# The first layernorm of sequences 1 to 15 taken from transposed input instead of through TensorE

## The chip, the cores and the metric

The kernel runs on one core of one Trainium2 chip. The metric is the device time of one launch in microseconds (us). The kernel before was timed in three runs: 996.58 us median, 995.12 us lowest, 997.07 us highest.

## The reference

The reference is a block of a conditioned transformer on 16 sequences of 256 tokens with 256 channels, in float32, with 16 heads of 64 and 8 experts of width 1024. Cut to what matters:

```python
def _ln(x, g, b):
    m = jnp.mean(x, axis=-1, keepdims=True)
    v = jnp.var(x, axis=-1, keepdims=True)
    return (x - m) * jax.lax.rsqrt(v + EPS) * g + b
shift = silu(t) @ W_ada.T + b_ada
h = _ln(x, ln1_g, ln1_b) + shift            # the first layernorm
qkv = (h @ Wqkv.T).reshape(b, n, 3, H, HD)
q, k = _ln(q-part, qn_g, qn_b), _ln(k-part, kn_g, kn_b)   # per head
attn = softmax(q @ k.T / sqrt(HD))
x = x + (attn @ v) @ Wout.T
tok = x.reshape(-1, d)
gate = softmax(tok @ Wgate.T)
vals, idx = top_k(gate.T, bs // E)          # each expert takes 512 tokens
g = _ln(tok[idx], mlp_g, mlp_b)
y = gelu(g @ fc1 + b1) @ fc2 + b2
tok = tok.at[idx].add(y * w)
```

The change concerns the line of `h` alone: the mean and the rate 1/sqrt(v + EPS) belong to a token, the gain `ln1_g` and the shift (`ln1_b` plus `shift`) to a channel.

## The kernel before, in words

**Stages.** The first part of the program works through the 16 sequences; the second routes tokens to experts and runs the experts' two matmuls, job by job. In the first part every sequence needs its normalised input `hT` with channels on partitions (two chunks of 128 channels, 256 tokens each), since TensorE contracts over partitions. From `hT` come the q, k and v rows in six groups of 512 columns for two halves of 128 tokens (`Group`, tile `pm`). Then come the normalisation of q and k on ScalarE, VectorE and GpSimd, their turn into channel order, the scores (`Quad.scores`, tile `sc`), the exponentials, their normalisation on GpSimd (`Quad.normalise`, tile `pr`), a turn of 32x32 blocks on VectorE (`pb`) with four DMAs that deal the blocks to partitions (`exchange`, tile `prT`), the product with v (`po`), and the output projection with the gate logits (`Tail.project`, tile `pw`).

**The first layernorm before** is the class `First`. VectorE takes mean and variance of the 256 channels of a token (L639, L640, tokens on partitions, input `xs`). GpSimd raises variance plus EPS to the power -1/2 (L644, and `rsqrt` at L102). VectorE applies both (L651, tile `xn`). TensorE turns the result in four 128x128 blocks (L660, into a PSUM tile `ph` with the tag "mm", of which there are three tiles for `pm`, `ph`, `pq`, `pw` and half of `po`). ScalarE evicts it with gain and shift of the channel into `hT` (L673). A tile `xT`, the raw input with channels on partitions, is loaded as well, for the gate logits in `Tail.project`; there are two such tiles.

**Shapes of the array.** TensorE runs in three shapes. `halved` (L496 to L500) splits a 128x128 weight into two 128x64 halves, for `pm`, `pw` and the like; `product` (L920) uses 128x64 too; `scores` (L834) uses quarters of 64x64; transposes use all 128x128. Except in transposes, every float32 matmul of the program shows as two records in the trace, so 16 rows of the program's order are 32 records.

**The order.** The program is written as a list of steps (`plan.step`, called `at`): a nominal place, an engine, a duration, the function, what it needs and makes, and the tiles it holds. A table of numbers, `PLACES`, one for each step, fixes the order in which all steps are issued (`Plan.order`, used at L1800). Each engine and each DMA queue works through its own steps strictly in that order, and each instruction waits for what it needs. The SyncE queue (SP) issues the loads of `xs` and `xT`, the exchanges and the stores of the tokens.

Of the kernel before, what the change touches and what calls it, by code (L numbers as in the profile page):

```python
# [63 lines left out]
def kernel(  # L64
# [115 lines left out]
    def make_others():  # L180
# [287 lines left out]
    if True:  # L468
# [161 lines left out]
        class First:  # L630
# [18 lines left out]
            def apply(self, t):  # L649
                self.xn[t] = work.tile([P, D], F32, tag="xn", bufs=4, name="xn")  # L650
                nc.vector.tensor_scalar(  # L651
                    self.xn[t], xs[self.b][:, t, :], self.mv[:, 0, t : t + 1],
                    self.rs[:, 1, t : t + 1], ALU.subtract, ALU.mult,
                )

            def transposes(self):
                self.pt = turned_in("ph", self.b == 0)
# [1287 lines left out]
```

## Time and profile before

| | |
|---|---|
| median of three runs | 996.58 us |
| the profiled execution's own time | 994.14 us |
| its span, first to last instruction | 992.3 us |
| PE (TensorE) busy | 974.5 us, 98% |
| DVE (VectorE) busy | 788.0 us, 79% |
| POOL (GpSimd) busy | 652.3 us, 66% |
| ACT (ScalarE) busy | 595.1 us, 60% |

The span ends 1.84 us short of the profiled execution's time. That execution is 2.44 us below the median of the runs. Shares are of the whole span; the two parts of the program load the engines differently, so they are read by stretch. In the listings, matmuls overlap their neighbours, so what a group costs TensorE is read from the distance between the start of one group and the start of the next, rather than from the busy time of the group.

### The profile page before, as it was taken

How to read it: one execution, taken by the hardware profiler on the slowest of the kernel's cores; microseconds unless marked ns; L12 is line 12 of the kernel's file. 1: busy time of each engine (PE TensorE's matmuls, PEld its weight loads, DVE VectorE, ACT ScalarE, POOL GpSimd, SP SyncE). 2: the span in 40 equal slices, each digit the busy share in tenths (PEclk: the TensorE clock that was granted, in tenths of full speed). 3: DMA queues.
4: the chain of work that ended last, by engine and by line, in shares of the span. 5: the costliest groups of instructions: out<-in, count | busy, mean ns of one | idle time of the engine just before them, and what ended most of it. 6: DMA issues, size and time to landing. Idle time of an engine off the chain costs nothing.

```text
span 992.3 us, 22827 instructions
## 1 busy us (share of the span) xinstructions
PE 974.5 (98%) x7732; PEld 583.4 (59%) x7732; DVE 788.0 (79%) x1919; ACT 595.1 (60%) x1684; POOL 652.3 (66%) x1069
## 2 busy tenths in 40 slices
PE   9999999999999999999999999999999999999996
PEld 5444544444454545444454544455577888899995
DVE  6788888988899899898899899989964666477661
ACT  2788675757766676666667676766773432344441
POOL 4688677768687767777676777776535345455653
PEclk9999999999999999999999999999999999999998
DMA  8024567667576776576676667777734665766672
GB/s 289 1 55 96 139 155 170 153 166 189 144 176 166 185 189 164 127 174 172 162 179 160 170 156 184 179 176 178 180 108 145 212 181 160 218 187 183 196 220 31
DMA packets 153667, 160.56 MB, mean 162 GB/s; under 512 B 16080, under 2 KB 146640, under 8 KB 153552
## 3 DMA queue, kind: packets, MB, share of 16 engines
q1 hardware_dynamic: 145152, 148.68, 55.6%
q0 software_dynamic: 7168, 8.53, 5.1%
q10 hardware_dynamic: 1232, 1.90, 0.6%
q8 instruction: 62, 1.02, 0.4%
q14 instruction: 53, 0.43, 0.1%
HBM read 53.94 MB, written 12.84 MB: 67 GB/s over the span
## 4 chain that ended last, share of the span: by engine, by line
PE 82%; POOL 5%; DVE 4%; DMA 3%; issue 2%; SPq 2%; ACT 1%; POOLq 0%; DVEq 0%
PE pm L500 28%; PE ph L1427 10%; PE po L920 10%; PE sc L834 10%; PE pw L500 9%; PE seven L1483 5%; PE py L1443 5%; POOL ss L102 2%; DMA prT<-pb 2%; SPq L594 1%; POOL pr L867 1%; PE pp L898 1%; PE ph L660 1%; PE fill L489 1%; PE px L1396 1%
## 5 line engine op out<-in xcount | busy, mean ns | idle before, releaser
L500 PE MATMUL pm<-wq,hT 128*64 128x512 f32 x1536 | 350.6, 595 | 1.0 <-DVE qk L749 0.6
L867 POOL TENSOR_SCALAR pr<-pr,sums 128x256 f32<-128x256 f32 x512 | 236.8, 480 | 81.0 <-DVE sums L863 69.3
L856 ACT ACTIVATE pr<-sc,nmax 128x256 f32<-128x256 f32 x512 | 237.4, 479 | 84.3 <-DVE nmax L843 69.0
L102 POOL TENSOR_TENSOR ss<-ss,neghalf 128x8 f32<-128x8 f32 x128 | 210.4, 1644 | 10.6
L500 PEld LDWEIGHTS pm<-wq,hT 128*64 128x64 f32 x1536 | 108.1, 137 | 181.5 <-issue 153.2
L843 DVE TENSOR_REDUCE nmax<-sc 128x2 f32<-128x512 f32 x256 | 166.3, 669 | 6.5 <-PE sc L834 6.0
L877 DVE STREAM_TRANSPOSE pb<-pr 128x512 f32<-128x512 f32 x232 | 156.7, 690 | 16.1 <-POOL pr L867 8.8
L725 ACT ACTIVATE sq<-pm 128x512 f32<-128x512 f32 x128 | 77.0, 603 | 86.9 <-PE pm L500 83.9
L920 PE MATMUL po<-prT,v 128*64 128x256 f32 x1024 | 126.1, 381 | 1.6 <-DMA prT<-pb 1.2
L834 PE MATMUL sc<-kT,qT 64*64 64x256 f32 x2048 | 126.6, 383 | 0.1
L500 PE MATMUL pw<-wo,oT 128*64 128x264 f32 x1024 | 126.2, 389 | 0.2
L1427 PE MATMUL ph<-xT,w 128*128 128x256 f32 x512 | 117.2, 383 | 0.8 <-ACT xT L1414 0.7
L920 PEld LDWEIGHTS po<-prT,v 128*64 128x64 f32 x1024 | 73.3, 137 | 63.3 <-issue 28.1
L856 ACT ACTIVATION_READ_ACCUMULATOR pr<-sc,nmax 128x1 f32 x512 | 108.0, 211 | 0.0
L834 PEld LDWEIGHTS sc<-kT,qT 64*64 64x64 f32 x2048 | 72.5, 132 | 60.3 <-issue 21.6
L749 DVE TENSOR_TENSOR qk<-pm,ss 128x512 f32<-128x512 f32 x128 | 90.0, 704 | 19.1 <-POOL ss L102 17.9
L729 DVE TENSOR_REDUCE ss<-sq 128x8 f32<-128x512 f32 x128 | 85.5, 669 | 24.7 <-ACT sq L725 23.8
L1427 PEld LDWEIGHTS ph<-xT,w 128*128 128x128 f32 x512 | 94.2, 190 | 13.9 <-ACT xT L1414 1.6
L1434 ACT ACTIVATE hid<-ph,few 128x256 f32<-128x256 f32 x128 | 60.2, 473 | 66.0 <-PE ph L1427 61.8
L500 PEld LDWEIGHTS pw<-wo,oT 128*64 128x64 f32 x1024 | 71.3, 137 | 38.6 <-issue 5.2
L1377 POOL DMA_INDIRECT xg<-xn_dram,idx x32 | 33.7, 1054 | 85.6 <-DVE idx L1370 31.2
L781 DVE STREAM_TRANSPOSE kb<-qk 128x512 f32<-128x512 f32 x120 | 82.8, 693 | 1.8 <-DMA prT<-pb 0.6
(212 smaller groups left out, 1112.0 us busy)
## 6 DMA issues: line engine op xcount, KB each, us to landing
prT<-pb SPq DMA_DIRECT2D x464, 128.0 KB, 2.6
w<-in_fc2T SPq DMA_DIRECT2D x16, 1024.0 KB, 6.2
w<-in_fc1T SPq DMA_DIRECT2D x16, 1024.0 KB, 9.1
qraw<-kb SPq DMA_DIRECT2D x120, 128.0 KB, 2.6
kT<-kb SPq DMA_DIRECT2D x120, 128.0 KB, 2.7
xs<-in_x SPq DMA_DIRECT2D x16, 256.0 KB, 3.3
xT<-in_xT SPq DMA_DIRECT2D x16, 256.0 KB, 3.2
out<-tok SPq DMA_DIRECT2D x32, 128.0 KB, 2.5
```

The source lines that it names most:

```text
L102: nc.gpsimd.tensor_tensor(dst, src, neghalf[:, : src.shape[1]], ALU.pow)
L500: nc.tensor.matmul(dst[half], weights[:, half], moving, start=start, stop=stop)
L729: nc.vector.tensor_reduce(self.ss[:, 0, :], self.sq.rearrange("p (q e d) -> p e q d", q=QB, e=8), AX.XY, ALU.add,)
L749: engine.tensor_tensor(dst, src.rearrange("p (q e d) -> p q e d", q=QB, e=8), by_head(self.ss[:, 1, :]), ALU.mult,)
L781: nc.vector.transpose(kb[0][:, :, self.t], self.qk.rearrange("p (q h d) -> p q h d", q=QB, d=SQ),)
L834: nc.tensor.matmul(self.sc[i, j][k * HD : (k + 1) * HD, t, :], qTs[self.b][rows, hp, bass.ts(2 * t + k, HD)], keys[rows, hp] if direct els ...
L843: nc.vector.tensor_reduce(self.nmax[i, j], self.sc[i, j], AX.X, ALU.max, negate=True)
L856: nc.scalar.activation(dst, src, AF.Exp, bias=self.nmax[i, j][:, t : t + 1], scale=1.0, accum_out=self.sums[i][:, 0, j, t : t + 1],)
L867: nc.gpsimd.tensor_scalar(self.pr[i, j][:, t, :], self.pr[i, j][:, t, :], self.sums[i][:, 1, j, t : t + 1], 1.0, ALU.mult, ALU.mult,)
L877: nc.vector.transpose(self.pb[i][:, :, :, j].rearrange("p k c t n -> p t k c n"), self.pr[i, j].rearrange("p t (k c m) -> p t k c m", c=TB ...
L920: nc.tensor.matmul(self.po[j * HD : (j + 1) * HD, i, :], vs[self.b][:, c, bass.ts(4 * self.d + 2 * i + j, HD)], prT[:, j, c] if self.whole ...
L1427: nc.tensor.matmul(self.ph[f], self.w1[:, c, bass.ts(f, P)], self.xT[:, c, :], start=(c == 0), stop=(c == DC - 1),)
```

## The change

For sequences 1 to 15 (sequence 0 keeps the old way) `First` no longer applies mean and rate with tokens on partitions, and TensorE no longer turns the result. Instead:

- GpSimd multiplies mean and rate of each token (`rates`, 128x2).
- VectorE transposes the four columns (mean times rate and rate, for two halves of the tokens), each repeated 32 times, in 32x32 blocks (`lay`, 128x128): every partition of a block of 32 then holds the values of that block's 32 tokens.
- SP deals each of the four blocks of 32 partitions to all 128 partitions by a DMA (`spread`, four per sequence, 64 KB written each).
- GpSimd multiplies `xT` by the rates (`times`) and subtracts mean times rate (`less`), each in two halves of 128x256 elements, into `hT`.
- ScalarE applies gain and shift in place (`shifted`, two instructions of 128x256).

`xT` is loaded earlier and has four tiles instead of two. The PSUM tile `ph` of sequences 1 to 15 is gone, as is the tag "xn" (`xn` of sequence 0 shares the tag "tok"). The table `PLACES` is new throughout, because there are more steps and another order.

```diff
@@ PLACES
-        0, 1, 2, 3, 4, 5, 6, 7, 18, 15, 21, 24, 23, 27, 31, 20, 14, 8, 56, 72, 73, 74, 75,
...
@@ class First
             def apply(self, t):
-                self.xn[t] = work.tile([P, D], F32, tag="xn", bufs=4, name="xn")
+                self.xn[t] = work.tile([P, D], F32, tag="tok", bufs=3, name="xn")
...
+            def rates(self):
+                nc.gpsimd.tensor_tensor(self.rs[:, 0], self.mv[:, 0], self.rs[:, 1], ALU.mult)
+            def lay(self):
+                self.side = work.tile([P, 2 * TB, SQ], F32, tag="side", bufs=2, name="side")
+                nc.vector.transpose(
+                    self.side,
+                    self.rs.rearrange("p k t -> p (k t)").unsqueeze(2).to_broadcast([P, 2 * TB, SQ]),
+                )
+            def spread(self, q):
+                if q == 0:
+                    self.rows = seq.tile([P, QB, 2 * TB * SQ], F32, tag="rows", bufs=2, name="rows")
+                part = self.side[q * SQ : (q + 1) * SQ].rearrange("p w i -> p (w i)")
+                nc.sync.dma_start(
+                    self.rows[:, q], part.unsqueeze(1).to_broadcast([SQ, QB, 2 * TB * SQ])
+                )
+            def along(self, k, t):
+                rows = self.rows.rearrange("p q (k t i) -> p k t q i", k=2, t=TB)[:, k, t]
+                return rows.unsqueeze(1).to_broadcast([P, DC, QB, SQ])
+            def by_block(self, v, t):
+                return v[:, :, bass.ts(t, P)].rearrange("p c (q i) -> p c q i", q=QB)
+            def times(self, t):
+                nc.gpsimd.tensor_tensor(
+                    self.by_block(self.out(), t), self.by_block(xTs[self.b], t), self.along(1, t),
+                    ALU.mult,
+                )
+            def less(self, t):
+                h = self.by_block(self.out(), t)
+                nc.gpsimd.tensor_tensor(h, h, self.along(0, t), ALU.subtract)
+            def shifted(self):
+                h = self.out()
+                for c in range(DC):
+                    nc.scalar.activation(
+                        h[:, c, :], h[:, c, :], AF.Identity,
+                        bias=bias1[:, c, self.b : self.b + 1],
+                        scale=vec[:, LN1_G + c : LN1_G + c + 1],
+                    )
@@ class Tail
-                xTs[self.b] = seq.tile([P, DC, N], F32, tag="xT", bufs=2, name="xT")
+                xTs[self.b] = seq.tile([P, DC, N], F32, tag="xT", bufs=4, name="xT")
@@ the steps of a sequence
+            at(base + FIRST[0] - 19, "SP", 0.64, Tail(b, 0).load, (), [("xT", b)], [("xT", b)], lag=3.0)
...
-                at(base + FIRST[4], "ACT", 0.91, a.evict, [("ht", b), "bias1"], [("hT", b)], [pt, ("hT", b)], lag=0.22)
+                rows, hT = ("lines", b), ("hT", b)
+                at(base + FIRST[1] + 0.1, "POOL", 0.22, a.rates, [("fp", b)], [("fr", b)], [l1])
+                at(base + FIRST[1] + 0.2, "DVE", 0.2, a.lay, [("fr", b)], [("fl", b)], [l1, ("side", b)], lag=0.19)
+                for q in range(QB):
+                    at(base + FIRST[1] + 0.3 + 0.1 * q, "SP", 0.66, partial(a.spread, q), [("fl", b)] + ([("ls", b, q - 1)] if q else []), [rows, ("ls", b, q)], [("side", b), rows], lag=2.2)
+                for t in range(TB):
+                    at(base + FIRST[2] + t, "POOL", 0.68, partial(a.times, t), [rows, ("xT", b)], [("h1", b, t)], [rows, ("xT", b), hT])
+                    at(base + FIRST[2] + t + 0.5, "POOL", 0.68, partial(a.less, t), [("h1", b, t)], [("h2", b)], [rows, hT])
+                at(base + FIRST[4], "ACT", 0.98, a.shifted, [("h2", b), "bias1"], [hT], [hT], lag=0.22)
```

**The order on TensorE** around the scores of sequence 6 and the first scores of sequence 7. `ph` is the turn of sequence 7's normalised input; the numbers behind tile names are those of buffers. Before:

```order
L500 MATMUL pm<-wq,hT_3229 64x512 x16
L834 MATMUL sc<-kT_2886,qT_3092 64x256 x16
L920 MATMUL po<-prT,v_2914 64x256 x4
L500 MATMUL pm<-wq,hT_3229 64x512 x4
L920 MATMUL po<-prT,v_2914 64x256 x4
L500 MATMUL pw<-wo,oT_3330 64x264 x2
L500 MATMUL pw<-few,xT 64x8 x4
L500 MATMUL pw<-wo,oT_3330 64x264 x16
L500 MATMUL pw<-few,xT 64x8 x4
L500 MATMUL pw<-wo,oT_3330 64x264 x14
L660 MATMUL ph<-ident,xn 128x128 x4
L834 MATMUL sc<-kT_3585,qT_3719 64x256 x16
```

The same place with the change:

```order
L525 MATMUL pm<-wq,hT_2995 64x512 x16
L905 MATMUL sc<-kT_3010,qT_3001 64x256 x16
L525 MATMUL pw<-wo,oT_3185 64x264 x2
L525 MATMUL pw<-few,xT 64x8 x4
L525 MATMUL pw<-wo,oT_3185 64x264 x14
L525 MATMUL pm<-wq,hT_2995 64x512 x4
L525 MATMUL pw<-wo,oT_3185 64x264 x2
L525 MATMUL pw<-few,xT 64x8 x4
L525 MATMUL pw<-wo,oT_3185 64x264 x14
L991 MATMUL po<-prT,v_2959 64x256 x4
L905 MATMUL sc<-kT_3636,qT_3687 64x256 x16
```

The four transposes between `pw` and `sc` are gone and nothing has taken their place; the other rows are dealt differently. Elsewhere the new order splits groups of scores. This is sequence 3 with the change:

```order
L905 MATMUL sc<-kT_1903,qT_1968 64x256 x16
L525 MATMUL pm<-wq,hT_1595 64x512 x8
L991 MATMUL po<-prT,v_1206 64x256 x12
L905 MATMUL sc<-kT_1903,qT_1968 64x256 x8
L991 MATMUL po<-prT,v_1206 64x256 x4
L525 MATMUL pm<-wq,hT_1595 64x512 x16
```

A group of 16 there has become two of 8, with other work between them. Up to the first transpose of the routing (`pgT`), the order before has 64 uninterrupted groups of `sc`, two of which are of 8; the new order has 69, twelve of which are of 8. In the routing, six rows of `pw` stand between the first list (`pls`) and the 36 fills ahead of the first `px`, where before the fills came right behind the list.

**The order on GpSimd** around the input of sequence 4 (`hT_1595` with the change; `pr` are the probabilities, which the products wait for; `ss` and `rs` are small powers). With the change:

```order
L709 TENSOR_TENSOR hT_1595<-xT,rows 128x2x128
L636 TENSOR_SCALAR rs<-mv 128x1
L102 TENSOR_TENSOR rs<-rs,neghalf 128x1
L938 TENSOR_SCALAR pr<-pr,sums 128x256 x6
L806 TENSOR_SCALAR ss<-ss 128x8
L102 TENSOR_TENSOR ss<-ss,neghalf 128x8
L806 TENSOR_SCALAR ss<-ss 128x8
L102 TENSOR_TENSOR ss<-ss,neghalf 128x8
L938 TENSOR_SCALAR pr<-pr,sums 128x256 x2
L709 TENSOR_TENSOR hT_1595<-xT,rows 128x2x128
L938 TENSOR_SCALAR pr<-pr,sums 128x256 x2
L716 TENSOR_TENSOR hT_1595<-hT_1595,rows 128x2x128
```

Before, the queue holds probabilities and powers alone in these sequences:

```order
L735 TENSOR_SCALAR ss<-ss 128x8
L102 TENSOR_TENSOR ss<-ss,neghalf 128x8
L611 TENSOR_SCALAR rs<-mv 128x1
L102 TENSOR_TENSOR rs<-rs,neghalf 128x1
L867 TENSOR_SCALAR pr<-pr,sums 128x256 x4
```

The elementwise work on `hT` (L709, L716) now stands between the probabilities, in single pieces or in pairs.

**The order on the SP queue** of the same sequences with the change (`rows` are the dealt rates):

```order
L619 DMA prT<-pb 128x1x256 x4
L697 DMA rows<-side 128x1x128
L507 DMA xs_2884<-in_x 128x2x256
L1094 DMA xn_dram<-tn 128x256
L619 DMA prT<-pb 128x1x256 x4
L697 DMA rows<-side 128x1x128
L1015 DMA xT<-in_xT 128x2x256
L619 DMA qraw<-kb 128x1x256 x4
L697 DMA rows<-side 128x1x128 x2
L619 DMA prT<-pb 128x1x256 x4
```

Sixty issues of `rows` are new, dealt between the exchanges, and the loads of `xT` have moved to earlier places. The whole queue has 856 issues before and 916 with the change.

## Rows read from the trace of the kernel before

**Rows 1.** The page, part 1: busy time, share of the span, instructions.

```profile
PE 974.5 (98%) x7732; PEld 583.4 (59%) x7732; DVE 788.0 (79%) x1919; ACT 595.1 (60%) x1684; POOL 652.3 (66%) x1069
```

**Rows 2.** Windows: length, busy us per engine (instructions), PE clock, DMA share, GB/s.

```profile
60.00:700.00 640.00, 636.57 (x5428) 313.00 (x5426) 569.80 (x1152) 438.51 (x1302) 475.00 (x849) 1.00 0.65 163
...
709.00:753.00 44.00, 41.57 (x454) 29.62 (x455) 30.77 (x136) 28.99 (x94) 16.91 (x37) 1.00 0.41 120
```

**Rows 3.** Waits of PE: line waited for, total us, times, longest.

```profile
PE po L920 <- DMA prT<-pb: 1.2, 3, 0.7
...
PE pm L500 <- DVE qk L749: 0.6, 1, 0.6
PE ph L660 <- DVE gates L1026: 0.5, 1, 0.5
```

**Rows 4.** Timeline of PE near 140 us: start us, us, engine, line, operation, records.

```profile
136.30 3.63 PE L500 MATMUL pm<-wq,hT 128*64 128x512 f32 x16
139.86 0.65 PE L660 MATMUL ph<-ident,xn 128*128 128x128 f32 x4
140.44 1.96 PE L834 MATMUL sc<-kT,qT 64*64 64x256 f32 x32
142.33 1.08 PE L500 MATMUL pm<-wq,hT 128*64 128x512 f32 x4
```

**Rows 5.** Timeline of PE: 48 records of `pm` in a row; scores right behind 16.

```profile
10.32 10.52 PE L500 MATMUL pm<-wq,hT 128*64 128x512 f32 x48
20.67 0.40 PE L500 MATMUL pf<-few,wout 128*64 128x64 f32 x8
...
709.49 3.65 PE L500 MATMUL pm<-wq,hT 128*64 128x512 f32 x16
713.07 1.96 PE L834 MATMUL sc<-kT,qT 64*64 64x256 f32 x32
```

**Rows 6.** Timeline of PE near 86 us: a group of scores half as long.

```profile
85.73 1.09 PE L834 MATMUL sc<-kT,qT 64*64 64x256 f32 x16
86.76 1.08 PE L500 MATMUL pm<-wq,hT 128*64 128x512 f32 x4
```

**Rows 7.** Lines by form, PE: records, busy us, mean ns, idle before, releaser.

```profile
L660 PE MATMUL ph<-ident,xn 128*128 128x128 f32 x64 | 10.8, 294 | 0.5 <-DVE gates L1026 0.5
```

**Rows 8.** Lines by form, POOL.

```profile
L867 POOL TENSOR_SCALAR pr<-pr,sums 128x256 f32<-128x256 f32 x512 | 236.8, 480 | 81.0 <-DVE sums L863 69.3 <-DVE gates L1026 2.8 <-ACT v L721 0.9
L589 POOL TENSOR_TENSOR wq<-wq,ws 128x512 f32<-128x512 f32 x4 | 4.5, 1135 | 0.3
L989 POOL TENSOR_TENSOR tok<-tok,xs 128x256 f32<-128x256 f32 x4 | 2.8, 734 | 0.0
L1081 POOL TENSOR_TENSOR gates<-gates,smax 128x16 f32<-128x16 f32 x1 | 0.2, 212 | 5.3 <-DVE gate_of L1076 5.3
```

**Rows 9.** Lines by form, DVE and ACT.

```profile
L877 DVE STREAM_TRANSPOSE pb<-pr 128x512 f32<-128x512 f32 x232 | 156.7, 690 | 16.1 <-POOL pr L867 8.8 <-DMA qraw<-kb 3.4 <-DMA prT<-pb 2.2
L863 DVE RECIPROCAL sums<-sums 128x4 f32<-128x4 f32 x128 | 19.5, 154 | 7.4 <-ACT pr L856 6.9
L651 DVE TENSOR_SCALAR xn<-xs,mv,rs 128x256 f32<-128x256 f32 x32 | 13.1, 412 | 0.2 <-POOL rs L102 0.2
L673 ACT ACTIVATE hT<-ph,bias,few 128x256 f32<-128x256 f32 x31 | 16.0, 571 | 18.2 <-PE ph L660 18.2
```

**Rows 10.** Timeline of the SP queue near 302 us: four issues of an exchange.

```profile
301.67 2.50 SPq L594 DMA_DIRECT2D kT<-kb  x4
```

**Rows 11.** The page, parts 3 and 6: queue totals, and us to landing.

```profile
q1 hardware_dynamic: 145152, 148.68, 55.6%
...
prT<-pb SPq DMA_DIRECT2D x464, 128.0 KB, 2.6
```

**Rows 12.** Timeline of PE in the routing: `pgT` starts it, `ph` starts the experts.

```profile
708.85 0.71 PE L1109 MATMUL pgT<-ident,gate_of 128*128 128x128 f32 x2
...
733.68 1.56 PE L500 MATMUL pw<-wo,oT 128*64 128x264 f32 x12
735.05 0.38 PE L500 MATMUL pw<-few,xT 128*64 128x8 f32 x8
...
745.89 4.10 PE L489 MATMUL fill<-ident 128*128 128x128 f32 x36
750.18 0.41 PE L1396 MATMUL px<-ident,xg 128*128 128x128 f32 x2 [0.20 <-DMA xg<-xn_dram,idx]
751.34 0.44 PE L1396 MATMUL px<-ident,xg 128*128 128x128 f32 x2 [0.74 <-DMA xg<-xn_dram,idx]
...
752.57 3.72 PE L1427 MATMUL ph<-xT,w 128*128 128x256 f32 x16 [0.68 <-ACT xT L1414]
```

More of the change, by code (lines that the diff above doesn't have):

```diff
@@ L1546 @@
         plan = Plan(dict(
-            mm=3, sc=4, po=1, xs=5, hT=2, qT=2, kT=2, v=2, oT=2, xn=4, sq=2, ss=4, qk=3, nmax=8, aside=4,
-            sums=4, pr=PRB, pb=3, qraw=2, prT=4, tok=3, tn=2, xT=2, pa=1, l1=4, l2=4,
+            mm=3, sc=4, po=1, xs=5, hT=2, qT=2, kT=2, v=2, oT=2, lines=2, side=2, sq=2, ss=4, qk=3, nmax=8, aside=4,
+            sums=4, pr=PRB, pb=3, qraw=2, prT=4, tok=3, tn=2, xT=4, pa=1, l1=4, l2=4,
         ))
@@ L1591 @@
             at(base + FIRST[1], "POOL", 0.92, a.power, [("fs", b)], [("fp", b)], [l1])
-            for t in range(TB):
-                at(base + FIRST[2] + t, "DVE", 0.32, partial(a.apply, t), [("fp", b)], [("xn", b)], [l1, ("xs", b), ("xn", b, t)], lag=0.18)
-            pt = ("mm", b, 0)
-            at(base + FIRST[3], "PE", 0.44, a.transposes, [("xn", b)], [("ht", b)], [pt, ("xn", b, 0), ("xn", b, 1)] + ([("mm", b, 0.1)] if b == 0 else []), lag=0.22)
             if b == 0:
+                for t in range(TB):
+                    at(base + FIRST[2] + t, "DVE", 0.32, partial(a.apply, t), [("fp", b)], [("xn", b)], [l1, ("xs", b), ("tok", "xn", t)], lag=0.18)
+                pt, pt1 = ("mm", b, 0), ("mm", b, 0.1)
+                at(base + FIRST[3], "PE", 0.44, a.transposes, [("xn", b)], [("ht", b)], [pt, ("tok", "xn", 0), ("tok", "xn", 1), pt1], lag=0.22)
                 at(base + FIRST[4], "ACT", 0.56, partial(a.evict, (0,)), [("ht", b), "bias1", "later"], [("hT", b)], [pt, ("hT", b)], lag=0.22)
-                at(base + FIRST[4], "DVE", 0.42, partial(a.evict_too, 1), [("ht", b), "bias1"], [("hT", b)], [("mm", b, 0.1), ("hT", b)], lag=0.19)
+                at(base + FIRST[4], "DVE", 0.42, partial(a.evict_too, 1), [("ht", b), "bias1"], [("hT", b)], [pt1, ("hT", b)], lag=0.19)
             else:
-                at(base + FIRST[4], "ACT", 0.91, a.evict, [("ht", b), "bias1"], [("hT", b)], [pt, ("hT", b)], lag=0.22)
+                rows, hT = ("lines", b), ("hT", b)
[3 more added lines that the diff above has]
+                    at(base + FIRST[1] + 0.3 + 0.1 * q, "SP", 0.66, partial(a.spread, q), [("fl", b)] + ([("ls", b, q - 1)] if q else []), [rows, ("ls", b, q)], [("side", b), rows], lag=2.2)
+                for t in range(TB):
+                    at(base + FIRST[2] + t, "POOL", 0.68, partial(a.times, t), [rows, ("xT", b)], [("h1", b, t)], [rows, ("xT", b), hT])
+                    at(base + FIRST[2] + t + 0.5, "POOL", 0.68, partial(a.less, t), [("h1", b, t)], [("h2", b)], [rows, hT])
+                at(base + FIRST[4], "ACT", 0.98, a.shifted, [("h2", b), "bias1"], [hT], [hT], lag=0.22)
             turned = {g: [] for g in range(4)}
@@ L1669 @@
                 pw, tok, tn, l2 = (("sc", 97) if (b, t) == (B - 1, 1) else ("mm", 4)) + n, ("tok",) + n, ("tn",) + n, ("l2",) + n
-                if t == 0:
-                    at(p - 40, "SP", 0.65, a.load, (), [("xT", b)], [("xT", b)], lag=3.0)
                 need, tile_ = [("oT", b), ("xT", b), "wog"], [pw, ("oT", b), ("xT", b)]
```

486 rows, old and new, of the table PLACES are left out of this document.

## The prediction

> **What bounds the kernel now.** I read the busy shares first, then the windows by stage, then TensorE's waits, and last the timeline around the transposes that the change removes. The shares put TensorE at 98% of the span and the next engine, VectorE, at 79% [rows 1]. A share is no proof of a bound, so the stage that the change touches comes next: from 60 to 700 us TensorE is busy 636.57 of 640 us, VectorE 569.80, GpSimd 475.00 and ScalarE 438.51 [rows 2]. TensorE idles 3.4 us there, all at the full clock (1.00). Its waits in this stage are short and few: 1.2 us in three pieces for `prT`, 0.6 us for `qk`, 0.5 us ahead of one group of `ph` [rows 3]. So in the attention stage an operation taken off TensorE is time taken off the end, as long as the others keep up. From 709 to 753 us TensorE has 2.4 us idle and much fill work, and the search for the thresholds sets the pace [rows 2, 12]. That stage should move as a whole: it begins with `pgT`, when TensorE has got through the same attention work as before.
>
> **The transposes that go.** Fifteen groups of four leave TensorE's order. What one costs is read from starts. A `ph` group that starts at 139.86 is followed by scores at 140.44, which is 0.58 us [rows 4]. Ahead of it, 16 records of `pm` took 3.56 us from their start to `ph`; where scores follow 16 records of `pm` directly, it is 3.58 us [rows 4, 5]. So without the group the way into the scores costs the same as the way into the group did, and the whole 0.58 us is saved: 15 x 0.58 = 8.7 us. Bounds: the group of 64 has 10.8 us of busy time, of which 60/64 is 10.1, with ends that overlap the next work [rows 7]; and 36 fills, transposes of the same size in one run, take 4.10 us, 0.114 each, so 60 of them at that rate are 6.8 us [rows 12]. I take 8.7, since it was read at the place itself.
>
> **What the new order gives back on TensorE.** Scores stand in 64 uninterrupted groups before `pgT` in the old order and in 69 in the new one, so five more splits. A whole group takes 1.89 us to the start of the next work, half a group 1.03 [rows 4, 6]: two halves cost 2.06, 0.17 more. Entering scores costs something too: 48 records of `pm` in a row take 10.35 us, 0.216 each, so 16 should take 3.45, and took 3.58 before scores [rows 5]. That is 0.13 more per entry. Five splits at 0.30 are +1.5 us. The Trainium skill's page "TensorEngine Tiling (Array Packing)", section Key Properties, says that changing the tiling mode drains TensorE. The 0.13 and 0.17 us agree with it. The rule speaks against the new order, not against the removal: by it alone one would credit each removed group with a change of shape as well, 15 x 0.13 = 2.0 us more and a sum of -7.3 in place of the -5.3 below, while the rows show the entry into `ph` replaced by an equal entry into the scores.
>
> **GpSimd.** Per sequence come four two-input instructions of 128x256 and a small one. The nearest rows are 734 ns for 128x256, and 1135 ns for 128x512 with a broadcast operand, 568 for half of it [rows 8]. I take 0.65, between the two, and 0.21 for the small one [rows 8]: 2.8 us per sequence, 42 us in all (37 to 47). Nothing leaves GpSimd. Hence 475 of 640 us, 74%, becomes about 516 of 633, 82%. By itself this is beside TensorE; what it costs is lateness of `pr`, on which `pb`, the exchange and `po` hang, because pieces of `hT` now stand ahead of it in the queue.
>
> **VectorE and ScalarE.** VectorE loses two applications of 0.41 us per sequence and gains one block transpose of 128x128, bounded by 0.15 (the smallest instruction shown) and 0.69 (four times the elements); I take 0.3, nearer to the small one since it has a quarter of the elements [rows 9]. That is 0.5 us less per sequence on an engine at 89% in this stage, so nothing lost. ScalarE's two instructions of 0.57 us [rows 9] stay, reading SBUF instead of PSUM: no term, between -0.1 and +0.1 us each, and hidden, as ScalarE is at 69% there. One user of the three "mm" tiles goes, which can only relax TensorE; no term.
>
> **SP and the transfers.** Four more issues per sequence at 0.6 us (four took 2.50) are 2.4 us of SP's queue [rows 10], 36 us in all, hidden as long as exchanges behind them land in time. Each writes 64 KB; by packets of 512 B, 60 x 128 are 7,680 on top of 145,152, which took 55.6% [rows 11], so about 3 points more if a small packet costs as much as the mean one. An exchange lands in 2.6 us [rows 11]; I leave it there. The first DMA of `rows` waits for `lay`, and the exchanges of `prT` queue behind it. The earlier `xT` loads are the same bytes at other times; those of the first sequences stand ahead of some weights, which could cost up to about 1 us early on (256 KB; issue gaps of 0.6 us), taken as 0.
>
> **Waits that I add.** TensorE's idle time in the stage is 3.4 us now. GpSimd's busy time over its free time goes from 475/165 = 2.9 to 516/117 = 4.4, half as much again. If TensorE's idle time grows in proportion, that is +1.7; I take +1.6 us, an estimate, with 0 and 7 as bounds (7: half a microsecond in each of 15 sequences).
>
> **The routing.** Six rows of `pw`, 12 records, take 1.37 us [rows 12] and now stand ahead of the 36 fills, so the first `px` starts some 1.2 us later. The second waited for its gather at 751.34 anyway, and the experts start at 752.57 after it [rows 12]. I add 0.3 us, between 0 and 1.2.
>
> **The sum.** -8.7 + 1.5 + 1.6 + 0.3 = -5.3 us. Against the profiled execution's 994.14 (span 992.3 and 1.84 around it) this gives 988.8. The median of the runs shown is 2.44 above that execution, and I take the same distance for the changed kernel: 996.58 - 5.3 = 991.3 us. About 0.2%, 2 us, is what a measurement of this kernel can tell from no change.
>
> **Rivals.**
> - *Nothing new waits.* TensorE gets all of -8.7 + 1.5 = -7.2, or a little more if the freed "mm" tile removes some of the 3.4 us idle: 989.4, down to 987. For it: GpSimd itself stands idle 69.3 us for the sums before `pr` [rows 8]. Against: a fuller queue has less to spare. Chance 0.20.
> - *The hand-over gives it all back.* Exchanges queue behind a `rows` issue that waits for its `lay`; if the 2.4 us of such a set reach TensorE in three of fifteen sequences, that is 7.2, and the time is 996.6, no change. For it: `prT` is already TensorE's longest wait of this stage [rows 3]. Against: only 1.2 us of it in total. The case that VectorE is the true pace, at 89%, comes out here too. Chance 0.13.
> - *GpSimd becomes the bound: slower.* The place is `po`, behind `pr`. Four pieces of `hT` delay `pr` by 2.6 us per sequence; if more than 7.2/15 = 0.48 us of that reaches TensorE per sequence, the gain is gone, and with 1.0 us it is 15 - 7.2 + 0.3 = +8.1, or 1004.7 us. Against it: 82% leaves 18% free, and no wait of TensorE in the stage is put down to GpSimd now. The Trainium skill's "GPSIMD Engine Reference", section Performance versus the Vector engine, holds GpSimd to be the wrong engine for elementwise work, about half as fast as VectorE, with 4497 ns for 2048 elements of a two-input add. By that figure 256 elements are an estimated 0.56 us, near the lower of my bounds, and no row here shows the same instruction on both engines. Chance 0.08.
>
> That the change does not do what it says is excluded by the order: one of sixteen `ph` groups is left, and no other transposes replace them.
>
> **How the numbers follow.** The forecast of 991.3, with added waits between 1 and 4 us, has a chance of 0.59; it and the clean case are faster by over 0.2% (0.79). No change has 0.13, slower 0.08. The range runs from 987.0, the clean case with the larger saving by rows 7, to 997.0, which takes in the case that gives all back; it leaves out the slower rival and the far edges.
>
> **What would show it.** Right: `ph` of the first layernorm with 4 records; TensorE still over 99% busy between 60 and 700 us; `pgT` about 5 to 7 us earlier than 708.85, and the distance from `pgT` to the first expert matmul, 43.7 us now, within 1 us; elementwise `hT` at 0.57 to 0.73 us; GpSimd at about 82% in the stage. Wrong: idle TensorE ahead of `po` in most sequences, with `prT` or `pr` named; `pm` waiting for `hT`; elementwise instructions of over 1 us; or VectorE's block transposes growing beyond 0.69 us while GpSimd works on two inputs.

## The result, and the profile after

The changed kernel takes 1007.25 us (median of 4, 1006.36 to 1008.50) against 995.85 us before (median of 4 in the same comparison, 994.43 to 997.07): a ratio of 1.0116, 95% interval 1.0096 to 1.0136. So it is 11.4 us slower, where 5.3 us less were forecast. The profiled execution took 1006.57 us, with a span of 1004.9 us, 12.6 more than before.

The busy shares and the windows by stage of the changed kernel (length, busy us of each engine with its instructions, granted clock, DMA share, GB/s):

```profile
PE 975.8 (97%) x7672; PEld 577.2 (57%) x7672; DVE 781.0 (78%) x1904; ACT 597.2 (59%) x1684; POOL 699.2 (70%) x1144
```

```profile
0.00:60.00 60.00, 55.38 (x386) 27.41 (x390) 36.52 (x74) 29.89 (x69) 37.75 (x63) 0.97 0.41 138
60.00:700.00 640.00, 633.61 (x5370) 306.02 (x5364) 564.08 (x1135) 440.13 (x1299) 516.25 (x912) 1.00 0.68 167
...
709.00:753.00 44.00, 42.10 (x468) 28.99 (x465) 31.07 (x138) 29.38 (x99) 16.23 (x37) 1.00 0.39 113
```

The stage from 60 to 700 us looks as forecast: TensorE is at 99.0%, GpSimd at 81%, VectorE 5.7 us lower than in [rows 2]. The added instructions have nearly the sizes taken (0.73 us for 0.65 on GpSimd, 0.29 for 0.3 on VectorE). Lines by form, GpSimd and then VectorE:

```profile
L709 POOL TENSOR_TENSOR hT<-xT,rows 128x256 f32<-128x256 f32 x30 | 21.8, 733 | 5.4 <-DMA rows<-side 2.7 <-DMA xT<-in_xT 2.0 <-issue 0.7
L716 POOL TENSOR_TENSOR hT<-hT,rows 128x256 f32<-128x256 f32 x30 | 21.8, 730 | 0.8
```

```profile
L688 DVE STREAM_TRANSPOSE side<-rs 128x128 f32<-128x128 f32 x15 | 4.3, 288 | 1.9 <-POOL rs L683 1.9
```

Yet `pgT`, forecast 5 to 7 us earlier than 708.85, starts at 711.45. The span splits into four parts, before and after: to `pgT` 708.85 and 711.45 (+2.6); on to the first `pls` 36.9 and 37.7 (+0.8); on to the first expert matmul 6.8 and 11.2 (+4.4); on to the end 239.8 and 244.6 (+4.8).

Three places show in TensorE's timeline (start us, us, engine, line, operation, records, idle before and its releaser):

```profile
29.41 3.63 PE L525 MATMUL pm<-wq,hT 128*64 128x512 f32 x8 [2.21 <-ACT hT L721]
...
750.81 4.15 PE L514 MATMUL fill<-ident 128*128 128x128 f32 x36
758.53 0.44 PE L1467 MATMUL px<-ident,xg 128*128 128x128 f32 x2 [3.56 <-DMA xg<-xn_dram,idx]
...
760.28 8.68 PE L1498 MATMUL ph<-xT,w 128*128 128x256 f32 x32 [0.33 <-ACT xT L1485]
...
782.81 0.29 PE L1424 MATMUL pls<-ranked,row 128*128 128x130 bf16 x2 [1.59 <-DVE row L1414]
```

Behind each of these idle times TensorE's granted clock falls to 1.2 GHz for a stretch, which happens nowhere in mid-run of the kernel before (windows: length, PE busy, granted clock, DMA share, GB/s; means of under 1.00 are mixtures of 1.0 and 0.5):

```profile
28.00:33.00 5.00, 3.59 (x9) 0.66 0.01 2
...
760.00:764.00 4.00, 3.72 (x10) 0.58 0.10 33
...
783.00:787.00 4.00, 3.84 (x13) 0.60 1.03 381
```

Each costs 1.6 to 1.7 us: 5 x 0.34, 4 x 0.42, 4 x 0.40.

**A sum behind the busy share.** For every kernel I added up, over TensorE's matmuls before `pgT`, the distance from each start to the next. From each I took off the usual distance for that pair of tiles in that place of a run of matmuls (the 35th percentile over all kernels here). The usual distances are TensorE's own time; what is left are its waits, also those that hide inside a "busy" matmul. The recipe needs pairs that most kernels have: where only one kernel has a pair, its waits pass for own time. Before: 690.4 own and 17.0 waits. After: 682.6 and 27.4. So TensorE's own time fell by 7.8 us (forecast: 8.7 - 1.5 = 7.2), and the waits grew by 10.4 (forecast: 1.6), 3.3 of it before 80 us.

### The profile page after: what moved, and what is told of

The parts are those of the page before. It is cut to its first block, busy times and chain, and to the rows that moved or that the text cites. A ratio compares the mean times of both kernels' runs of the same rounds, so it can differ in the third digit from the quotient of the medians.

```text
span 1004.9 us, 22878 instructions
## 1 busy us (share of the span) xinstructions
PE 975.8 (97%) x7672; PEld 577.2 (57%) x7672; DVE 781.0 (78%) x1904; ACT 597.2 (59%) x1684; POOL 699.2 (70%) x1144
## 5 line engine op out<-in xcount | busy, mean ns | idle before, releaser
L905 PE MATMUL sc<-kT,qT 64*64 64x256 f32 x2048 | 129.4, 384 | 1.2 <-ACT pr L927 0.7
L1498 PE MATMUL ph<-xT,w 128*128 128x256 f32 x512 | 120.5, 391 | 0.5 <-ACT xT L1485 0.3
```

The source lines that it names most:

```text
L905: nc.tensor.matmul(self.sc[i, j][k * HD : (k + 1) * HD, t, :], qTs[self.b][rows, hp, bass.ts(2 * t + k, HD)], keys[rows, hp] if direct els ...
L1498: nc.tensor.matmul(self.ph[f], self.w1[:, c, bass.ts(f, P)], self.xT[:, c, :], start=(c == 0), stop=(c == DC - 1),)
```

## The experiments

### Behind `pgT`: the second expert's weights

In the change, six `pw` rows stand behind `pls`, and SyncE loads the second expert's weights as soon as these rows have freed a tile. SyncE's and GpSimd's timelines of the change:

```profile
750.92 0.38 SPq L1403 DMA_DIRECT2D w<-in_fc2T  x1
751.35 0.58 SPq L1405 DMA_DIRECT2D w<-in_fc1T  x1
```

```profile
750.29 1.27 POOL L1448 DMA_INDIRECT xg<-xn_dram,idx  x1 [11.15 <-DVE off L1431]
751.87 0.96 POOL L1448 DMA_INDIRECT xg<-xn_dram,idx  x1 [0.30 <-DVE idx L1441]
```

2 MB leave just ahead of the second gather, which lands at 758.5, 6.6 us after its issue. Before the change GpSimd's timeline has it at 748.52, SyncE's has the weights at 750.71, and `px` started behind it at 751.34 [rows 12], 2.8 us after its issue.

**Weights later.** One line: `places[3470] = 3467.5` in place of 3466 puts the load behind the next store in SyncE's order.

> Only the load of the second expert's weights is put two places later in the queue of SyncE, behind the store that waits for GpSimd's add. Theory A (those 2 MB go out 0.5 us ahead of the second gather and make it 6.6 us long, TensorE waits 3.6 us for it and then runs 3.4 us at half clock, which costs 1.7 us): the second gather lands within 3.5 us, the wait ahead of px is under 0.5 us, no half-clock spell at 760, and the time falls by about 5 us, from 1007 to 1002. Rival B (the six late pw rows and the late token behind them are the loss, the gather is only a witness): the time stays within 1.5 us of 1007.

Measured: 998.55 us, 1.0036 of before (1.0021 to 1.0052). `pls` to the first expert matmul takes 7.4 us instead of 11.2, and the rest 241.0 instead of 244.6. SyncE, TensorE, and the windows of the two former half-clock stretches:

```profile
752.99 0.34 SPq L1042 DMA_DIRECT2D out<-tok  x1
753.43 0.38 SPq L1403 DMA_DIRECT2D w<-in_fc2T  x1
```

```profile
754.16 0.38 PE L1467 MATMUL px<-ident,xg 128*128 128x128 f32 x2
```

```profile
760.00:764.00 4.00, 3.95 (x20) 1.00 0.56 193
...
783.00:787.00 4.00, 4.00 (x22) 1.00 0.33 48
```

Theory A holds, and gave more than it foresaw: `px` waits for no gather, and both half-clock stretches are gone, the second too, though `pls` still waits its 1.6 us for `row`.

**Rows earlier, and both edits.** `places[3334..3337] = 3400.5, 3405.5, 3419.5, 3428.5` spreads the late rows between the counts again; the second kernel has the weights later as well.

> Only the late pw rows of token tile 30 go back to places between the counts, as before the change. Theory A (what hurts is where the weights leave): the weights are freed some 5 us earlier still, leave at about 746, collide with the first gather or with both, so that a wait of 1 to 4 us stays ahead of px; what is won is the later part (the wait for row of 1.6 us and the half-clock spell after it, together 3 us): 1002 to 1005. Rival B (the late rows are the loss): all of the 10 us between pgT and the end comes back, about 997.

> Both edits: the late pw rows back between the counts, and the weights behind the store. Theory A: the whole loss after pgT (10 us) comes back, no half-clock spell behind pgT, about 997, and the first expert matmul stands within 1 us of 43.7 us behind pgT. If something else in the new order makes the end late (the order of tiles 30 and 31 on ScalarE and GpSimd), it stays above 1000.

Measured: 1004.80 us, 1.0093 (1.0067 to 1.0120), and 1003.22 us, 1.0079 (1.0048 to 1.0109). With the rows alone the time is what Theory A said: the weights leave at 748.49, ahead of both gathers, and `px` waits as long as in the change:

```profile
758.46 0.60 PE L1467 MATMUL px<-ident,xg 128*128 128x128 f32 x2 [3.56 <-DMA xg<-xn_dram,idx]
```

Both together are no better than the weights alone. My expectation of 997 was wrong: rows ahead of the threshold make `pls` 1.1 us later (38.8 us behind `pgT`), and they no longer cover the time until the gather has landed, so `px` waits 1.4 us and two half-clock stretches come back. The late place of the rows is right; the harm was in what it set free.

### The start

**Sequence 1 the old way**, with `if self.b == 1:` in the new steps and its normalisation and transposes put at `places` 57.3 to 74.5.

> Sequence 1 alone takes the old way through TensorE (normalised on VectorE, 4 transposes, evicted by ScalarE); sequences 2 to 15 as in the change. Theory A (the first stall is the new way's latency at the start: rows landed at 25.9, input ready at 29.9, TensorE there at 27.2): the wait of 2.2 us at 29.4 and the half-clock spell behind it (1.7 us) go, 0.6 us of transposes is added: 1007.2 - 3.3 = 1004. Rival (the start is short of weights, not of the input): the wait moves to another matmul and the time stays within 1 us of 1007.

**Rates before loads:** `places[446] = 64.5`, and the weights later.

> The load of the second expert's weights behind the store, as in the run that moved it alone (998.6 us), and the load of sequence 2's transposed input behind the fourth transfer of sequence 1's rates instead of ahead of it. The fourth transfer was issued at 21.5 and landed at 25.95, when GpSimd began; it should be issued at about 19.6 and land at 24, so that sequence 1's input is ready at 28 and TensorE, there at 27.2, waits 0.5 to 1 us instead of 2.2, without the half-clock spell: 2 to 3 us less, 996 to 997. If the landing is bound by the loads in flight, nothing moves: 998 to 999.

**Weights later and sequence 1 the old way.**

> Both repairs that worked, together: the second expert's weights behind the store, and sequence 1 on the old way. If the two add up: 998.6 - 2 = 996.5, within 0.3% of the kernel before. If the start's gain is swallowed by waits behind it (its pgT was only 0.9 us earlier), 997.5 to 998.5.

Measured: 1004.28 us, 1.0084 (1.0062 to 1.0106); 1002.39 us, 1.0057 (1.0040 to 1.0074); 1000.55 us, 1.0041 (1.0026 to 1.0057). In the first and third the wait at 29.4 and its half-clock stretch are gone, and the first scores start 1.5 and 1.9 us earlier. But `pgT` stands at 710.6, only 0.9 us earlier than in the change, and at 711.0, against 710.8 with the weights moved alone. Most of what the start wins is lost again further on, so the first kernel's 1004, which Theory A had as a number, is not shown to come from its reason. In the second, the fourth transfer is issued about 2 us earlier and the rows still come only half a microsecond sooner than at 25.95. The loads in flight may bound it, as the expectation had it; this run shows only that the place of the issue does not:

```profile
25.43 1.42 POOL L709 TENSOR_TENSOR hT<-xT,rows 128x256 f32<-128x256 f32 x2 [2.50 <-DMA rows<-side]
```

The second kernel's time is above both cases of its expectation. `pgT` (711.3) does not explain that; the stretch behind the first expert matmul does, with 244.2 us where the weights moved alone have 241.0. TensorE waits for the experts' `xT` there, 2.1 us in three pieces, against 0.3 in one. Why is open; the third kernel's tail is long as well (243.5).

### Way or order

> The new way of the first layernorm (sequences 2 to 15; sequence 1 keeps the old way) in the order of the kernel before: every step that both kernels have stands where it stood before, the new steps are put in behind the statistics of their sequence, the elementwise passes ahead of where ScalarE's eviction stood, and no group of scores is split anew. Theory A (the new order is what loses, the way itself saves its transposes): pgT 14 times 0.58 us earlier than 708.85, that is 700.7, plus at most 3 us of waits; the stretch behind pgT as before the change; about 987 to 990 in all. Rival B (GpSimd's four passes, the rows' transfers or VectorE's transposes make TensorE wait wherever they stand): pgT at 707 to 712, and no faster than 994.

```diff
-        for k in plan.order(PLACES):
+        places = (
...
+        )
+        for k in plan.order(places):
```

> The reverse: the order of the change, but all sequences on the old way (normalised on VectorE, 4 transposes on TensorE each, evicted by ScalarE). Theory A (the order loses): the transposes come on top of the change's pgT of 711.4, at 717 to 719, and with the late end as in the change about 1013. Rival B (the new way loses, the order is harmless): pgT at 708 to 710, and about 1004, all of it behind pgT.

The edit is cut here: the other new steps return as well, and the transposes get places of their own.

```diff
             def times(self, t):
+                if self.b:
+                    return self.apply(t)
...
             def less(self, t):
+                if self.b:
+                    return self.transposes() if t == 0 else None
...
             def shifted(self):
+                if self.b:
+                    return self.evict()
```

Measured: 1031.64 us, 1.0354 (1.0326 to 1.0381), and 1015.95 us, 1.0196 (1.0171 to 1.0222). The new way in the old order goes beyond both theories: `pgT` at 740.7 and 57.5 us of waits. The way needs an order of its own (I tried one set of places for its steps). TensorE's longest waits there (line waited for, us, times, longest):

```profile
PE sc L915 <- ACT pr L937: 5.3, 6, 1.7
PE pm L525 <- DVE gates L1107: 4.7, 3, 2.4
PE po L1001 <- DMA prT<-pb: 4.4, 4, 1.4
```

The old way in the new order has `pgT` at 717.2, as Theory A said, but the run does not show its reason. The sum gives this kernel 18.7 us of waits and 697.0 of TensorE's own time, 14.4 more than the change; fifteen groups of transposes at 0.58 are 8.7. Here the sum misleads. Ten of the fifteen groups take 0.56 to 0.59 us to the next start. Behind the other five stands a `pm`, and it starts 0.5 to 1.2 us later than a `pm` behind such a group otherwise does, 4.4 us in all. TensorE's timeline has these as waits, three for `hT` and two for `qk`:

```profile
389.49 0.66 PE L741 MATMUL ph<-ident,xn 128*128 128x128 f32 x4
391.26 1.94 PE L525 MATMUL pm<-wq,hT 128*64 128x512 f32 x8 [1.11 <-ACT hT L754]
```

So its waits are some 23 us, against 17.0 before and 27.4 in the change, and part of them comes from the places that I gave the transposes. The two kernels do not divide the loss between the way and the order. The next ones do, since all of them keep TensorE's order of the change.

### Which part of the new way waits

**GpSimd's passes:** multiplied twice over, the subtraction left out (`return` in `less`), both left out (ScalarE's shift reads `xTs[self.b]`).

> GpSimd multiplies by the rates twice over (two more passes of 0.73 us for each of 15 sequences, 22 us of GpSimd in all); nothing else differs from the change. If GpSimd paces the attention, pgT is 5 to 22 us later than 711.4. If it has room, pgT moves by under 2 us, and the waits of the change are not of GpSimd's load.

> Left out: the subtraction of the mean times rate (30 of the 60 elementwise passes, 22 us of GpSimd); the input of sequences 1 to 15 keeps its mean. If GpSimd's load makes the attention's waits, pgT comes 3 to 7 us earlier than 711.4 (704 to 708). If the order does, pgT stays within 1.5 us; the wait of 2.2 us at the start shortens by 1.5 in either case.

> Left out: both elementwise passes (all 60 of GpSimd); ScalarE's shift and scale reads the loaded transposed input instead, so sequences 1 to 15 enter without their normalisation. The rates, VectorE's turn in blocks and the four transfers of each sequence stay. The waits of TensorE up to pgT, taken as the sum over its matmuls of the distance from start to start less the usual distance in that place, were 16.9 us before, 27.0 in the change, 25.1 without the subtraction, 18.3 with the old way in the change's order. If the passes make the added waits: pgT 702 to 705 and waits of 17 to 20 us. If the turn, the transfers or the shift make them: pgT 706 to 709 and waits of 22 to 25 us, with the start's 3 us gone in either case.

**Turn and transfers:** `return` in `lay` and in `spread`, or in one of them; the passes then read a constant tile, or the transfers carry one.

> Left out: VectorE's turn in blocks and the 60 transfers; the elementwise passes read a constant tile instead of the rates, so sequences 1 to 15 enter without their own normalisation. If the turn or the transfers make the added waits (SyncE's queue, the landing), pgT comes 4 to 7 us earlier than 711.4; if GpSimd's passes do, only the start's wait for the rows goes, 1 to 3 us, and pgT is at 708 to 710.5.

> Left out: the 60 transfers alone; VectorE still turns the rates, GpSimd's passes read a constant tile (sequences 1 to 15 enter without their own normalisation). Theory S (the transfers load SyncE's queue, behind which the exchanges of prT, kT and qraw wait: its idle time between 60 and 700 us fell from 199 to 134 us with them and is 195 without turn and transfers): idle of SyncE about 195 us, pgT at 704 to 706 as without both. Theory V (VectorE's turn makes the waits): pgT at 709 to 711.

> The reverse: VectorE's turn left out, the 60 transfers kept (they carry a constant, so sequences 1 to 15 enter without their own normalisation). Theory S: SyncE's idle time between 60 and 700 us stays near 134 us and pgT at 709 to 712. Theory V: pgT at 704 to 706.

**Transfers that nobody waits for:** all of them go out, the passes read a constant tile (and `rows` has one buffer instead of two).

> VectorE's turn and all 60 transfers as in the change, but GpSimd's passes read a constant tile instead of the rows that land, so that nothing waits for the transfers (sequences 1 to 15 enter without their own normalisation). If SyncE's time is what they cost: its idle between 60 and 700 us at about 134 us, pgT at 709 to 712 with the start's 2 us taken off. If the waiting for their landing is: SyncE as busy, but pgT at 702 to 705, as in the run that left the transfers out.

Measured, with the ratio to before, the waits up to `pgT`, and SyncE's idle time from 60 to 700 us (what lies inside this window of the waits of its queue; the expectations count one long wait whole that began before it, and so have 199 and 134 for before and the change):

| kernel | passes | turns | transfers | ratio | `pgT` | waits | SyncE idle |
|---|---|---|---|---|---|---|---|
| before | - | - | - | 1 | 708.8 | 17.0 | 155 |
| the change | 60 | 15 | 60 | 1.0116 | 711.4 | 27.4 | 114 |
| twice | 90 | 15 | 60 | 1.0258 | 725.0 | 41.0 | 133 |
| no subtraction | 30 | 15 | 60 | 1.0090 | 709.6 | 25.5 | 117 |
| no passes | 0 | 15 | 60 | 1.0094 | 708.5 | 24.4 | 107 |
| no turn, no transfers | 60 | 0 | 0 | 1.0053 | 705.0 | 21.0 | 152 |
| turn alone | 60 | 15 | 0 | 1.0063 | 702.4 | 18.4 | 154 |
| transfers alone | 60 | 0 | 60 | 1.0129 | 712.1 | 28.1 | 114 |
| transfers unread | 60 | 15 | 60 | 1.0104 | 709.3 | 25.2 | 120 |

The intervals reach 0.0017 to 0.0027 to either side; all changed kernels keep the late gather, so `pgT` tells more than the ratio. A `pgT` is that of one profiled execution, and without the turn it is 2.6 us later than with the turn alone, so differences of 2 to 3 us are not read. Against the expectations: 90 passes came out as if GpSimd set the pace, the subtraction left out fell between its two cases, the turn alone has `pgT` 1.6 us earlier than either theory had it, and the others came out on the side of the transfers. Every kernel in which the 60 transfers leave through SyncE has 24 us of waits or more, with the passes or without; both that send none have 18 and 21. The transfers are enough without the turn, and they are enough when nobody reads them.

The start can be taken out. In all eight changed kernels TensorE's matmuls have the same order, so I counted from one and the same matmul of `sc` (at 80.27 us in the change) to `pgT`: 631.2 us in the change, 631.1 without the subtraction, 631.9 without passes, 632.1 with the transfers alone and 631.8 with them unread; but 626.7 with neither turn nor transfers and 624.1 with the turn alone. So behind the start the transfers cost 4 to 8 us, whatever the number of passes up to 60.

SyncE's longest waits for work, from 60 to 700 us: the change, then the turn alone.

```profile
SPq L619 <- DVE pb L948: 38.1, 31, 3.8
SPq L619 <- DVE ss L800: 35.1, 6, 25.5
SPq L619 <- DVE kb L852: 31.5, 17, 10.3
```

```profile
SPq L620 <- DVE ss L804: 60.7, 6, 46.8
SPq L620 <- DVE pb L952: 58.1, 46, 3.8
SPq L620 <- DVE kb L856: 41.9, 20, 10.3
```

Most of these are times at which SyncE had caught up and stood waiting for VectorE. The longest wait in either list began before the window, at 40.2 us (25.5) and at 17.0 us (46.8), and the table counts only its end. The 52 transfers of this stretch take 40 us of SyncE's idle (154 - 114), 0.8 us each, little more than the 0.6 us of an issue. What that does to an exchange can be read as well: from the end of its second `pb` to its first issue pass on average 0.9 us before, 1.2 with the turn alone, and 1.5 to 1.6 in the change, with the transfers alone and with them unread (some 112 exchanges, 80 to 700 us). An exchange is no slower once it is issued (DMA issues of the transfers alone, 60 to 700 us: times, KB, median us to landing):

```profile
prT<-pb SPq DMA_DIRECT2D x448, 128.0 KB, 2.6
...
rows<-level SPq DMA_DIRECT2D x52, 64.0 KB, 2.2
```

That is the 2.6 us of [rows 11]; the mean is 2.81 us here and 2.77 with the turn alone. So the transfers delay the exchanges by their turn in SyncE's queue, not on their way. That this delay is what TensorE waits for is likely and not shown: it is spread over many small waits. VectorE's waits for an exchange ahead of `pb` were one candidate (2.2 us before, 5.1 in the change, 10.4 with the transfers unread), but they are 4.0 us with the turn alone and 5.0 with neither turn nor transfers.

GpSimd is not out of it: 30 passes more cost 13.6 us of `pgT`, 11.1 of them behind the start, though 60 fewer give only 3.0, and none of that behind the start. The way is `qk`, which VectorE scales with GpSimd's `ss`, and which frees the tile for `pm`. In the kernel with 90 passes it becomes TensorE's longest wait:

```profile
PE pm L525 <- DVE qk L821: 7.4, 9, 2.1
PE pm L525 <- ACT hT L722: 5.9, 2, 4.4
```

### Another queue, and fewer transfers

**ScalarE's queue:** `nc.scalar.dma_start` in `spread`, and the weights later.

> The whole computation again: the 60 transfers are issued from ScalarE's queue instead of SyncE's, and the load of the second expert's weights stands behind the store. Theory S: SyncE's idle is back at about 195 us, pgT at 704 to 708, and the time 3 to 6 us below the run with the load moved alone (1.0036 of before): 0.998 to 1.000 of before. If the issues (0.6 us each, 36 us in all) cost ScalarE as much as they cost SyncE, whose place they take between the exponentials: pgT at 710 or later and 1.003 or more.

**Two transfers through DRAM**, with sequence 1 the old way and the weights later; the second stands at least 16.5 places behind the first:

```diff
+                if q == 0:
+                    self.line = dram.tile([QB, 2 * TB * SQ], F32, name=f"line{self.b}")
+                    side = self.side.rearrange("(q i) w n -> q i (w n)", q=QB)[:, 0]
+                    nc.sync.dma_start(self.line, side)
+                if q == 3:
...
+                    line = self.line.rearrange("q n -> (q n)").unsqueeze(0)
+                    nc.sync.dma_start(
+                        self.rows.rearrange("p q n -> p (q n)"), line.to_broadcast([P, QB * 2 * TB * SQ])
+                    )
```

> The whole computation, with two transfers for each of sequences 2 to 15 in place of four: the turned rates go to DRAM as one row (4 lines of 512 B), and come back to all partitions as one row of 2 KB each; the second is issued where the fourth stood. Sequence 1 on the old way, the second expert's weights behind the store. Theory S by count: SyncE's idle time between 60 and 700 us at about 165 us, half of the 9 us back, pgT at 706 to 708, and 0.997 to 1.001 of before. If the rows, one landing later (about 2.5 us), reach GpSimd too late: pm waits for hT, pgT at 711 or later, 1.003 or more.

**The same, with sequence 11's passes later** (`places[2310..2313] = 2063.1, 2070.5, 2052.1, 2052.2`).

> As the run with two transfers, and in sequence 11 GpSimd's four passes stand a normalisation later in its order, so that it does not stand waiting for the rows with the normalisation behind it. If the wait of 3.2 us and the half clock behind it were of that place alone: pgT at 705.5 to 707.5 (710.2 with them), 3 to 5 us less than 998.1, that is 0.998 to 1.001 of before. If another wait comes in its place: pgT at 709 or later, 1.002 or more.

Measured: 1008.50 us, 1.0158 (1.0135 to 1.0182); 998.09 us, 1.0033 (1.0017 to 1.0050); 997.68 us, 1.0035 (1.0017 to 1.0052). On ScalarE's queue SyncE's idle is back (164 us), but `pgT` stands at 719.6 with 35.5 us of waits: ScalarE, in order, stands behind its own issues, and the exponentials behind it, three times for 2.6 to 4.9 us.

```profile
ACT pr L927 <- DMA rows<-side: 10.4, 3, 4.9
```

With two transfers SyncE has 135 us of idle, an exchange is issued 1.3 us behind its `pb` on average, and `pgT` is at 710.2. One wait stands out in that trace, behind rows that came 3.0 us late to GpSimd in sequence 11:

```profile
462.05 3.46 PE L525 MATMUL pm<-wq,hT 128*64 128x512 f32 x8 [3.19 <-DVE qk L834]
```

The last kernel has no such wait, and `pgT` at 711.4 all the same, with 25.9 us of waits. So half the transfers gave back half of SyncE's lost idle (21 of 40 us) and most of the exchanges' delay, and nothing of the time that can be told. Why not is open, and it is why the last step, from the queue to TensorE, stays unproven; the rows also come later by this way. The range in which kernels with one and the same attention part (the change, and the three with edits behind `pgT`) put `pgT` is 710.8 to 711.9. ScalarE's queue and the last kernel came out as the second case of their expectations; the kernel between them has a `pgT` between its two cases. No version here is faster than the kernel before; the nearest are these two and the one with the weights moved alone, which is one line.

## Why the prediction was wrong

- **The transposes and the splits held.** -8.7 + 1.5 = -7.2 was forecast for TensorE's own time, -7.8 came. The Trainium skill's page "TensorEngine Tiling (Array Packing)", section Key Properties, would have had -9.2 if each removed group were credited with a change of shape; the trace is nearer to the rows' value. The miss is elsewhere: of the 17.9 us between the forecast (-5.3) and the span (+12.6), 8.8 are waits ahead of `pgT`, 8.9 the routing and 0.8 the way from `pgT` to `pls`, less 0.6 by which TensorE's own time came out better.
- **The step that failed first is that of SP and the transfers:** "four more issues per sequence ... hidden as long as exchanges behind them land in time". The count was nearly right: 36 us of the queue for 60 were forecast, and 52 took 40. But their cost was taken as 0, and with all passes in place `pgT` is at 709 to 712 with them and at 702 to 705 without: 4 to 10 us, and 4 to 8 without the start. The packets, 8,640 for 7,680 forecast, raised the queue's share of the DMA engines by 1.3 points and not by 3. The issues were not hidden: the exchanges behind them are issued later. The second rival had the mechanism, a hand-over that gives all back, with 7.2 us and a chance of 0.13; its own words, a `rows` issue that waits for `lay`, were not the cause, since the transfers alone, without a turn, cost as much. The Trainium skill's page "DMA: Bandwidth & Descriptors", section Issuing engines are not separate DMA queues, calls the time of an issue usually small relative to the transfer. Here it is 0.6 us against 2.2 to landing, and the runs speak against leaving it out: with the transfers alone the exchanges landed in 2.6 us as before and were issued later.
- **The waits were scaled by the wrong engine.** +1.6 us came from GpSimd's busy over its free time. With passes and turns but no transfers the waits are 18.4 against 17.0 (21.0 without the turns), so for GpSimd alone 1.6 was about right; for the whole way it was +10.4. The sign I named, TensorE over 99% busy, did not show it: it was 99.0%, since much of the waiting stands inside matmuls that count as busy.
- **The routing was +0.3 and was about +9** (4.4 + 4.8 us behind `pls`). I looked at what the six rows take and what covers it, not at what their end sets free: a tile, a load of 2 MB, and its place ahead of a gather. Moving that load gave back 7.4 us behind `pls`, 3.4 of which are the two half-clock stretches.
- **The start was 0** ("up to about 1 us"). It showed a wait of 2.2 us and 1.7 us of half clock; the repair brought less than 1 us at `pgT`, so most of it was lost again further on.
- **The third rival, GpSimd as the bound,** gave the right sign and nearly the size (+8.1 forecast, +11.4 measured) by luck: at 60 passes the runs do not bear out its reason. They do at 90.

## What to carry to other kernels

An operation that leaves the busiest engine is worth its time there only after each queue that the replacement passes through has been charged: here 60 small transfers, hidden by any sum of bytes, took a quarter of the slack of the one queue through which all exchanges go. When a step is put later, ask what its end frees, and which large transfer then starts in front of a small one that is waited for. And read waits from the distance between starts, since a busy share of 99% can hold 10 us of them; and look at the places that only one kernel has, where such a sum takes a wait for work.

## What was not expected of the hardware

- The second half-clock stretch behind `pgT` went away with the first, while the idle time that it followed (1.6 us ahead of `pls`) stayed. An idle time is not always followed by the lower clock.
- A transfer of 64 KB between partitions took 0.6 us to issue, 2.2 us to land and 0.8 us of its queue's slack. With half as many transfers, through DRAM, half of the slack came back (21 of 40 us), and the time did not.
